# The down projection of the first feed-forward split a second time from its third block on, in a two-layer gated block on one Trainium2 core

## The chip, the cores and the metric

The kernel runs on one core of one Trainium2 chip, as one program with one launch. The metric is the device time of that core in microseconds (us). The core has a matrix engine (TensorE, PE in the profile), a vector engine (VectorE, DVE), an activation engine (ScalarE, ACT), a general one (GpSimd, POOL), and SyncE (SP), which here only issues DMA transfers. The engines run their own instruction streams, each in its order, and wait for each other through semaphores. Matrix products go into PSUM[...]; everything else lies in SBUF or, larger things, in the chip's main memory (HBM).

## The reference

The input x has 8 sequences of 512 tokens with 512 features, all in fp32. Four residual steps follow each other, each on a layer norm of x and each scaled by a learned gate:

```
x = x + tanh(g_xattn[0]) * linear_attention(layernorm(x), ctx)     # 16 heads, gated, projections 512x512
x = x + tanh(g_ffn[0])   * ffn(layernorm(x))
x = x + tanh(g_xattn[1]) * cross_attention(layernorm(x), ctx, mask)
x = x + tanh(g_ffn[1])   * experts(layernorm(x))

ffn:      h = gelu(x @ proj1.T + proj1_bias)      # 512 -> 2048
          out = h @ proj2.T + proj2_bias          # 2048 -> 512, the down projection
experts:  8 groups of a gated feed-forward, 512 -> 2 x 1536 (gate and up), silu(gate) * up,
          weighted per token by a router, then 1536 -> 512
```

All matrix products have to be as good as fp32 ones. TensorE passes each fp32 matmul twice, and the profile counts both instructions.

## The kernel before, in words

A block is one sequence of 512 tokens. The program goes through all 8 blocks of the linear attention (to about 398 us), then through the 8 blocks of the first feed-forward (`ff0`), then through the 8 blocks of cross-attention and experts (`ff1`). Between the phases each block's x goes out to HBM and comes back.

**Seven products instead of eight.** Every large matrix product is cut into 2 x 2 quarters and computed by the Strassen-Winograd scheme: seven products of sums of quarters, joined by additions. The sums on the weights' side are made once, before the phase that needs them, by a builder on POOL (`combining`, L232, four subtractions per weight tile of seven parts), and stored to HBM. The sums on the activations' side are made per block on DVE.

- An *Up unit* (`Up`, L733) takes 512 hidden features: seven products in the order 1,2,6,5,7,4,3 (`ORDER`), each 4 matmuls of 128x256 output (8 instructions, 1.73 us) with one weight tile of 256 KB. Four units make one block of `ff0`, six one of `ff1`. The matmuls are on L754.
- `Down` (L855) is the down projection of `ff0`: seven products of 16 matmuls of 128x256 (32 instructions, L870) and four weight tiles each. Its results are added onto x by DVE straight from PSUM (L886), one part of 256 tokens x 256 features at a time. `after` also makes one more sum, s2 (L889).
- `SplitDown` (L893) is the down projection of `ff1`. It cuts each of the seven products a second time into seven, so there are 49 inner products, each over three chunks of 128 rows: 21 matmuls of 128x128 output (42 instructions, L941) per outer product. `combine` (L924) makes the four inner sums of an outer operand on DVE, each of 128x384. The seven inner results of an outer product lie in two PSUM banks, four in the first and three in the second. They are first summed over the outer products (ACT copies on L957 and L958, DVE additions on L963) into `sums`, and `whole` joins the inner sums at the end of the block (three additions on L989, eight gated additions onto x on L993).

The last products of each unit (from the sixth of an Up unit and the seventh of a down projection on) are run after the first product of the next unit (`steps`, L1123), so that PE has work while other engines finish.

**Banks.** Five accumulation banks are handed out from a list, `idle_banks`; three further banks serve transposes and the like. A product's letter (x, w, z, v in the profile's names) says which accumulator it uses; products 1 and 6 of a down projection use the same one.

**Weights and queues.** All weights stream from HBM through a ring of 16 tiles of 256 KB (`load_steps`, L1284), as transfers on SP's queue; a tile is loaded again as soon as PE has read it. SP issues in program order during both feed-forwards' first part (L1343), whereas the order of the other engines' instructions is chosen by the scheduler that builds the program; from the first block of `ff1` on no engine is bound to the program's order. `load_x` brings in the x of the block after next, also on SP, at the 20th product of a block (L1405); stores of x go out on ACT's queue.

**Normalization of the next block.** Statistics on DVE (L404, L405), the reciprocal root on POOL (rstd, L411), the scaling on DVE (xn, L420), transposes on PE (L427) and copies by ACT (L430) are done piecewise during a block for the next one; then four sums S on DVE (L539 to L542). POOL adds the second bias to x (L550).

**The builder during `ff0`.** While `ff0` runs, a generator (`build_weights("ff1")`, L347, and in its wake `build_stream`, L372) makes the weights of `ff1`. One step is taken after every fourth product of a block:

```
        if k % 4 == 0:
            next(builder, None)
```

Its pool `build` has two tiles of seven parts (L1345). A step issues loads on SP, or one POOL operation, or the stores on SP. For the twice split weights each of three chunks needs a second tile, and the result goes to `stream`, in the order in which the matmuls will read it.

Of the kernel before, what the change touches and what calls it, by code (L numbers as in the profile page):

```python
# [30 lines left out]
P = 128  # L31
# [37 lines left out]
def flamingo_kernel(  # L69
# [212 lines left out]
    SPLIT_ORDER = (2, 4, 1, 6, 5, 7, 3)  # L282
    SPLIT_INNER = (1, 2, 4, 5, 6, 7, 3)
    SPLIT_CHUNKS = NJ // 4
    stream = dram.tile([P, 7, 7, SPLIT_CHUNKS, P], F32, tag="stream", name="stream")
# [61 lines left out]
    def build_weights(ph, tile7):  # L347

        todo = {
            "ff0": (("up", raw_p1, 4), ("down", raw_p2, 4)),  # L350
            "ff1": (("up", raw_gu, 6),),
        }[ph]
        todo = [(kind, raw, i) for kind, raw, n in todo for i in range(n)]

        def load(kind, raw, i):
            t = tile7(f"{ph}_{kind}{i}")
            raw(t, i)
            return t

        t = load(*todo[0])  # L360
        yield
        for n, (kind, raw, i) in enumerate(todo):
            following = load(*todo[n + 1]) if n + 1 < len(todo) else None
            yield from combining(nc.gpsimd, t)
            for q in range(7):
                nc.sync.dma_start(out=store[ph, kind, i, q], in_=t[q])
            yield
            t = following
        if ph == "ff1":
            yield from build_stream(tile7)  # L370

    def build_stream(tile7):  # L372
        place = [SPLIT_ORDER.index(m) for m in (1, 5, 2, 3, 6, 7, 4)]
        for i in range(SPLIT_CHUNKS):
            t = tile7(f"ff1_down{i}")
            w = [t[k] for k in place]
            raw_dn(w, i)
            yield
            yield from combining(nc.gpsimd, w)

            t = buildp_view(t)
            more = buildp_view(tile7(f"ff1_split{i}"))
            m = {
                1: t[:, :, 0, 0], 5: t[:, :, 0, 1], 2: t[:, :, 1, 0], 3: t[:, :, 1, 1],
                6: more[:, :, 0, 0], 7: more[:, :, 0, 1], 4: more[:, :, 1, 0],
            }
            for dst, a, b in ((7, 3, 5), (5, 5, 1), (6, 3, 5), (4, 2, 6)):
                nc.gpsimd.tensor_tensor(m[dst], m[a], m[b], ALU.subtract)
                yield
            for n, k in enumerate(SPLIT_INNER):  # L390
                nc.sync.dma_start(out=stream[:, :, n, i, :], in_=m[k])
            yield

# [499 lines left out]
    class SplitDown(Unit):  # L893
# [4 lines left out]
        kind, i = "down", 0  # L898
        order, head = SPLIT_ORDER, 6
# [4 lines left out]
        def __init__(self, ph, b, chunks):  # L904
            self.ph, self.b, self.chunks, self.tag, self.banks = ph, b, chunks, f"{ph}_{b}_down", {}
            self.combined, self.numbers = {}, {}

        def step(self, m):
            name = self.BANK[m]
            if m in self.OPENS:  # L910
                two = [acc_bank(f"{name}{k}_{self.tag}") for k in range(2)]
                self.banks[name] = [t.rearrange("p n (h q) -> p (n h) q", q=P) for t, _ in two]
                self.numbers[name] = [n for _, n in two]
            self.product(m, self.banks[name])
            self.after(m, self.banks[name])
            if m in self.CLOSES:
                idle_banks.extend(self.numbers[name])

        def quarters(self, m):

            a = inner[self.NAMES[m]].rearrange("p (k n) (t q) -> p t n k q", n=2, q=P)
            return {f"{t + 1}{n + 1}": a[:, t, n] for t in range(2) for n in range(2)}

        def combine(self, m):  # L924

            a = self.quarters(m)
            s = second.tile([P, 4, self.chunks, P], F32, tag="split", name=f"split{m}_{self.tag}", bufs=2)
            nc.vector.tensor_tensor(s[:, 0], a["21"], a["22"], ALU.add)
            nc.vector.tensor_tensor(s[:, 1], s[:, 0], a["11"], ALU.subtract)
            nc.vector.tensor_tensor(s[:, 2], a["11"], a["21"], ALU.subtract)  # L930
            nc.vector.tensor_tensor(s[:, 3], a["12"], s[:, 1], ALU.subtract)
            self.combined[m] = s

        def product(self, m, p):
            a, s = self.quarters(m), self.combined.pop(m)
            w = ring_w[self.ph, self.kind, self.b]
            operand = {1: a["11"], 2: a["12"], 4: a["22"], 5: s[:, 0], 6: s[:, 1], 7: s[:, 2], 3: s[:, 3]}
            for n, k in enumerate(SPLIT_INNER):
                for c in range(self.chunks):
                    at = (SPLIT_ORDER.index(m) * 7 + n) * self.chunks + c  # L940
                    nc.tensor.matmul(  # L941
                        p[n // 4][:, n % 4, :],
                        lhsT=operand[k][:, c, :],
                        rhs=w[at // 4][:, ts(at % 4, P)],
                        start=m in self.OPENS and n % 4 == 0 and c == 0,
                        stop=True,
                        skip_group_check=True,
                    )

        def after(self, m, p):  # L950
            if m == SPLIT_ORDER[0]:
                t = second.tile([P, 7, 4, P], F32, tag="sums", name=f"sums_{self.tag}")
                self.sums = {(r + 1, c + 1): t[:, :, 2 * r + c, :] for r in range(2) for c in range(2)}
                self.all_sums = t

            def first(part):
                nc.scalar.copy(self.sums[part][:, 0:4], p[0])  # L957
                nc.scalar.copy(self.sums[part][:, 4:7], p[1][:, 0:3])  # L958

            def more(part):  # L960
                for at, src in ((slice(0, 4), p[0]), (slice(4, 7), p[1][:, 0:3])):
                    dst = self.sums[part][:, at]
                    nc.vector.tensor_tensor(dst, src, dst, ALU.add)  # L963

            if m in (2, 4, 6, 5):
                first({2: (1, 1), 4: (2, 1), 6: (1, 2), 5: (2, 2)}[m])
            if m == 7:
                more((2, 2))
                more((2, 1))
            if m in (1, 3):  # L970
                more({1: (1, 1), 3: (1, 2)}[m])
            if m == 6:
                nc.vector.tensor_tensor(inner["s2"], inner["a12"], inner["s2"], ALU.subtract)
            last = self.b == B - 1
            if m == 3:
                pending.extend(self.whole(0, 1) if last else self.whole(None, None))
            if m == 1 and last:
                pending.extend(self.whole(0, 0))
            if m == 7 and last:
                pending.extend(self.whole(1, None))  # L980

        def whole(self, r, c):

            x5 = xs[self.ph, self.b].rearrange("p (t r) (c h q) -> p t h (r c) q", t=2, c=2, q=P)
            at = slice(0, 4) if r is None else ts(r, 2) if c is None else ds(2 * r + c, 1)
            m = {k: self.all_sums[:, n, at] for n, k in enumerate(SPLIT_INNER)}

            def onto(k, by):
                return lambda: nc.vector.tensor_tensor(m[k], m[k], m[by], ALU.add)  # L989

            def out_of(k, t, h):
                dst = x5[:, t, h, at]
                return lambda: nc.vector.scalar_tensor_tensor(dst, m[k], GATE[self.ph], dst, ALU.mult, ALU.add)  # L993

            def done():
                if (r, c) in ((None, None), (0, 1)):
                    stores.append((self.ph, self.b))

            return [
                onto(6, 1), out_of(1, 0, 0), out_of(2, 0, 0), onto(5, 6), out_of(5, 0, 1), out_of(3, 0, 1),  # L1000
                out_of(5, 1, 1), out_of(7, 1, 1), onto(7, 6), out_of(7, 1, 0), out_of(4, 1, 0), done,
            ]
# [266 lines left out]
    def units_of(ph, b):  # L1269
        if ph == "ff0":  # L1270
            return [Ff0Up(ph, b, i) for i in range(4)] + [Down(ph, b, NF // 2)]
        return [Ff1Up(ph, b, i) for i in FF1_UNITS] + [SplitDown(ph, b, NJ // 4)]
# [11 lines left out]
    def load_steps():  # L1284
        for u, m, _ in plan:
            if isinstance(u, SplitDown):
                flat = stream.rearrange("p a b c q -> p (a b c q)")
                w = ring_w.setdefault((u.ph, u.kind, u.b), [])

                while 4 * len(w) < (SPLIT_ORDER.index(m) + 1) * 7 * SPLIT_CHUNKS:  # L1290
                    at = 4 * P * len(w)
                    t = ring(f"w_{u.ph}_{u.kind}_{u.b}_{len(w)}").rearrange("p n f -> p (n f)")
                    n = min(4 * P, 49 * SPLIT_CHUNKS * P - at)
# [12 lines left out]
    down_of = {u.b: u for u, _, _ in plan if isinstance(u, SplitDown)}  # L1306

    def tiles_of(u, m):

        if isinstance(u, SplitDown):  # L1310
            n, of = SPLIT_ORDER.index(m), 7 * SPLIT_CHUNKS
# [33 lines left out]
    buildp = build.enter_context(tc.tile_pool(name="build", bufs=2, reuse_waits="tile"))  # L1345

    seven = {}

    def build_tiles(name):
        t = buildp.tile([P, 7, 2, H2], F32, tag="build", name=f"build_{name}")  # L1350
        parts = [t[:, q] for q in range(7)]
        seven[id(parts[0])] = t
        return parts

    def buildp_view(parts):
        return seven[id(parts[0])].rearrange("p k n (h q) -> p k n h q", q=P)

    pick_experts()
    builder = build_weights("ff1", build_tiles)


# [5 lines left out]
    for u, m, n in plan:  # L1367
# [7 lines left out]
        if n == 2 * B and k == 0:  # L1375
            for _ in builder:
                pass
# [8 lines left out]
        if isinstance(u, Ff1Up) and u.i == FF1_UNITS[-1]:  # L1386

            if m in (2, 7):
                down_of[u.b].combine({2: 2, 7: 4}[m])
            if m == 3:  # L1390
                down_of[u.b].combine(1)
        if isinstance(u, SplitDown) and m in (4, 1, 6, 5, 7):
            u.combine(SPLIT_ORDER[SPLIT_ORDER.index(m) + 1])
# [5 lines left out]
        if k % 4 == 0:  # L1399
# [67 lines left out]
```

## Time and profile before

| | |
|---|---|
| time, median of 3 | 2124.71 us (2124.39 to 2125.57) |
| profiled execution | 2125.65 us |
| its span, first to last instruction | 2123.8 us |
| granted TensorE clock, mean | 0.995 |
| PE busy | 2088.8 us |
| DVE busy | 1238.9 us |
| ACT busy | 555.4 us |
| POOL busy | 251.5 us |
| DMA, mean over the span | 205 GB/s |

The span is the time from the first to the last instruction on the core in one profiled execution; the time is what the device reports for a whole execution, some 2 us more. "Busy" is the time in which an engine was at work on an instruction; loading weights (PEld) overlaps with the matmuls. A group of instructions is shown by its source line, engine, operation, and output and inputs by the program's names. Lines in the profile are lines of this kernel; where a helper records an operation, its line is L60.

### The profile page before, as it was taken

What the parts mean: (1) busy time and instruction counts of PE and PEld (TensorE: products, weight loads), DVE (VectorE), ACT (ScalarE), POOL (GpSimd) and SP (SyncE); (2) the same over time, 40 slices, a digit from 0 to 9 for tenths busy, and PEclk for the clock granted to TensorE, in tenths of its full rate; (3) what the DMA queues carried; (4) which work ended last, traced back from release to release, by engine and by line L of the source; (5) the groups of instructions that cost most, each with busy time, mean ns of one, the idle gap of its engine ahead of it and who ended that gap; (6) DMA issues with size and microseconds to landing.
All of it is one profiled execution on the core that took longest, in us unless ns stands there. A gap on an engine that the chain in (4) does not pass through costs nothing.

```text
span 2123.8 us, 30856 instructions
## 1 busy us (share of the span) xinstructions
PE 2088.8 (98%) x11452; PEld 1807.3 (85%) x11452; DVE 1238.9 (58%) x2289; ACT 555.4 (26%) x1146; POOL 251.5 (12%) x228
## 2 busy tenths in 40 slices
PE   8999999999999999999999999999999999999998
PEld 4778787788888888888888889898989889898988
DVE  3687787642333323242325278777777777876857
ACT  3433333222131303031324131212222222222121
POOL 3121111330111031030301010000000010100000
PEclk9999999999999999999999999999999999999999
DMA  7345633676666665575757658677776858585865
GB/s 224 120 154 161 201 129 101 214 252 212 216 211 204 222 207 187 175 242 170 245 164 237 198 164 277 196 249 224 217 247 185 284 167 293 162 282 160 269 203 164
DMA packets 258454, 434.84 MB, mean 205 GB/s; under 512 B 34305, under 2 KB 75937, under 8 KB 254209
## 3 DMA queue, kind: packets, MB, share of 16 engines
q1 hardware_dynamic: 250864, 406.10, 61.1%
q10 hardware_dynamic: 5856, 23.20, 3.0%
q0 software_dynamic: 1584, 3.57, 0.7%
q8 instruction: 92, 1.51, 0.3%
q14 instruction: 58, 0.47, 0.1%
HBM read 369.00 MB, written 63.77 MB: 204 GB/s over the span
## 4 chain that ended last, share of the span: by engine, by line
PE 82%; issue 8%; DMA 3%; DVE 3%; POOL 2%; SPq 1%; ACT 1%; POOLq 0%; ACTq 0%; DVEq 0%
PE x_ff L754 25%; PE w_ff L754 13%; PE x_ff_down L870 10%; PE z_ff L754 6%; PE x_ff_down L941 5%; PE w_ff_down L870 5%; PE w_ff_down L941 3%; PE z_ff_down L870 3%; PE v_ff_down L941 2%; PE z_ff_down L941 2%; PE pt_ff L427 1%; SPq L60 1%; PE pt_xa L427 1%; PE pr L620 1%; PE pst L578 1%
## 5 line engine op out<-in xcount | busy, mean ns | idle before, releaser
L766 ACT COPY u_ff<-x_ff 128x512 f32<-128x512 f32 x240 | 139.6, 582 | 773.0 <-PE x_ff L754 772.9
L754 PE MATMUL x_ff<-S_ff,w_ff_up 128*128 128x256 f32 x1280 | 304.7, 381 | 1.3 <-ACT u_ff L766 1.3
L754 PE MATMUL w_ff<-S_ff,w_ff_up 128*128 128x256 f32 x1280 | 303.9, 380 | 1.0 <-DVE a_ff L809 1.0
L754 PE MATMUL x_ff<-xnT_ff,w_ff_up 128*128 128x256 f32 x1280 | 293.2, 379 | 0.0
L754 PEld LDWEIGHTS x_ff<-S_ff,w_ff_up 128*128 128x128 f32 x1280 | 239.5, 190 | 46.0 <-issue 9.9
L754 PEld LDWEIGHTS w_ff<-S_ff,w_ff_up 128*128 128x128 f32 x1280 | 239.2, 190 | 33.3 <-issue 1.4
L754 PEld LDWEIGHTS x_ff<-xnT_ff,w_ff_up 128*128 128x128 f32 x1280 | 240.0, 190 | 32.3 <-issue 0.6
L870 PE MATMUL x_ff_down<-w_ff_down,a_ff 128*128 128x256 f32 x768 | 169.7, 379 | 0.0
L870 PEld LDWEIGHTS x_ff_down<-w_ff_down,a_ff 128*128 128x128 f32 x768 | 145.9, 190 | 19.9
L886 DVE SCALAR_TENSOR_TENSOR x_ff<-x_ff_down,gates,x_ff 128x512 f32<-128x512 f32 x32 | 24.0, 750 | 221.9 <-PE x_ff_down L870 216.4
L754 PE MATMUL z_ff<-xnT_ff,w_ff_up 128*128 128x256 f32 x640 | 151.5, 379 | 0.0
L754 PEld LDWEIGHTS z_ff<-xnT_ff,w_ff_up 128*128 128x128 f32 x640 | 119.8, 190 | 15.7 <-DMA w_ff_up<-ff_up 0.4
L870 PE MATMUL w_ff_down<-w_ff_down,s_ff 128*128 128x256 f32 x512 | 113.1, 379 | 0.0
L870 PEld LDWEIGHTS w_ff_down<-w_ff_down,s_ff 128*128 128x128 f32 x512 | 97.1, 190 | 13.1
L809 DVE TENSOR_TENSOR a_ff<-w_ff,u_ff 128x512 f32<-128x512 f32 x64 | 43.8, 685 | 91.9 <-ACT u_ff L766 89.8
L814 ACT ACTIVATE a_ff<-a_ff,b_sb 128x256 f32<-128x256 f32 x128 | 58.1, 500 | 95.4 <-DVE a_ff L809 95.2
L837 DVE SCALAR_TENSOR_TENSOR g_ff<-th_ff,x_ff 128x512 f32<-128x512 f32 x48 | 32.8, 684 | 83.6 <-ACT th_ff L836 83.6
L793 DVE TENSOR_TENSOR s_ff<-a_ff,a_ff 128x512 f32<-128x512 f32 x56 | 39.9, 712 | 68.0 <-ACT a_ff L814 67.8
L550 POOL TENSOR_TENSOR x_ff<-x_ff,b_sb 128x512 f32<-128x512 f32 x28 | 36.9, 1326 | 334.7 <-DVE xn_ff L420 334.7
L847 DVE TENSOR_TENSOR up_ff<-w_ff,u_ff 128x512 f32<-128x512 f32 x96 | 65.5, 682 | 18.2 <-ACT u_ff L766 18.2
L941 PE MATMUL x_ff_down<-w_ff_down,split_ff_down 128*128 128x128 f32 x576 | 69.9, 276 | 0.0
L839 DVE TENSOR_TENSOR g_ff<-g_ff,share 128x512 f32<-128x512 f32 x96 | 67.1, 699 | 2.1
(260 smaller groups left out, 3269.2 us busy)
## 6 DMA issues: line engine op xcount, KB each, us to landing
w_ff_up<-ff_up SPq DMA_DIRECT2D x560, 256.0 KB
w_ff_down<-stream SPq DMA_DIRECT2D x288, 256.0 KB
w_ff_down<-ff_down SPq DMA_DIRECT2D x224, 256.0 KB
x_ff<-x_ff SPq DMA_DIRECT2D x16, 1024.0 KB
share<-shares SPq DMA_DIRECT2D x64, 256.0 KB
ff_up<-build_ff_up SPq DMA_DIRECT2D x42, 256.0 KB
spread<-over SPq DMA_DIRECT2D x32, 256.0 KB
x_ff<-x_xa ACTq DMA_DIRECT2D x8, 1024.0 KB
```

Of the source, the lines that this page charges most:

```text
L427: nc.tensor.transpose(pt[:, c, :], xn[t][:, ts(c, P)], ident)
L550: nc.gpsimd.tensor_tensor(xb[:, t, :], xb[:, t, :], b2_sb, ALU.add)
L754: nc.tensor.matmul(p[:, n, :], lhsT=w[:, c, ts(n, P)], rhs=moving, **self.mark(m, 2 * n + c),)
L766: nc.scalar.copy(self.s[m], p)
L793: nc.vector.tensor_tensor(s1, a21, a22, ALU.add)
L809: nc.vector.tensor_tensor(h, p, s, ALU.add)
L814: nc.scalar.activation(h[:, n, :], p[:, n, :], AF.Gelu, bias=b1_sb[:, f : f + 1])
L837: nc.vector.scalar_tensor_tensor(g, th, 1.0, p, ALU.add, ALU.mult)
L839: nc.vector.tensor_tensor(g, g, share, ALU.mult)
L847: nc.vector.tensor_tensor(u, p, s, ALU.add)
L870: nc.tensor.matmul(p[:, t, :], lhsT=a[:, k, ts(t, P)], rhs=w[k // 2][:, k % 2, :], **self.mark(m, 2 * k + t),)
L941: nc.tensor.matmul(p[n // 4][:, n % 4, :], lhsT=operand[k][:, c, :], rhs=w[at // 4][:, ts(at % 4, P)], start=m in self.OPENS and n % 4 == ...
```

## The change

From the third block on (`ONCE = 2`), `ff0` uses `SplitDown` too. The class serves both phases, with its own order of outer products and number of chunks for each (four for `ff0`, three for `ff1`). In `ff0` an outer product is 28 matmuls of 128x128 (56 instructions), its inner sums are of 128x512, and a down projection reads 49 weight tiles of 256 KB where `Down` reads 28.

In `ff0` the seven inner results of an outer product are joined by themselves (`at_once`): ACT copies the two banks to two temporary tiles, DVE makes the joins in six additions, and one or two parts of x get the results by two gated additions each.

The weights for this, `stream["ff0"]`, are made during the first two blocks of `ff0` by a builder called `again`, one step after every second product; the builder of `ff1` follows it, one step after every fourth. Both now work in place, in one tile (`bufs=1`), with two POOL operations in a step (`in_twos`). The raw load of the next tile is issued when the stores of the one before have been issued.

The inner sums of an operand come from a pool of seven single tiles (`splits`) in place of two tiles of four. In both phases they are made one outer product ahead (`step`); for `ff1` this moves the sums of the first outer operands, which were made during the last Up unit.

The seven inner results have new places (`SPLIT_SLOT`): results 1, 6, 2 and 3 lie in the first bank, 4, 5 and 7 in the second, whereas the order in which they are computed stays 1,2,4,5,6,7,3. Joining in `ff1` uses the same six additions and two gated additions (`joined`), each over the four parts of x at once, where `whole` had three and eight.

```diff
-    SPLIT_ORDER = (2, 4, 1, 6, 5, 7, 3)
+    SPLIT_ORDER = {"ff0": (1, 4, 2, 6, 5, 7, 3), "ff1": (2, 4, 1, 6, 5, 7, 3)}
+    SPLIT_CHUNKS = {"ff0": NF // 4, "ff1": NJ // 4}
     SPLIT_INNER = (1, 2, 4, 5, 6, 7, 3)
+    SPLIT_SLOT = {1: 0, 6: 1, 2: 2, 3: 3, 4: 4, 5: 5, 7: 6}
+    ONCE = 2
...
+    def build_stream(ph, raw, tile7):
+        place = [SPLIT_ORDER[ph].index(m) for m in (1, 5, 2, 3, 6, 7, 4)]
+        for i in range(SPLIT_CHUNKS[ph]):
+            t = tile7(f"{ph}_down{i}")
+            w = [t[:, k] for k in place]
+            raw(w, i)
             yield
+            yield from in_twos(combining(nc.gpsimd, w))
...
+            for m, w in ((1, b11), (2, b21), (3, b22)):
+                keep(m, w)
             yield
+            nc.gpsimd.tensor_tensor(b12, b12, b11, sub)
+            keep(5, b12)
+            yield
+            nc.gpsimd.tensor_tensor(b22, b22, b12, sub)
+            keep(6, b22)
+            yield
+            nc.gpsimd.tensor_tensor(b21, b21, b22, sub)
+            nc.gpsimd.tensor_tensor(b11, b22, b11, sub)
+            keep(4, b21)
+            keep(7, b11)
+            yield
+        streamed.add(ph)
...
+            n = self.order.index(m) + 1
+            if n < 7:
+                self.combine(self.order[n])
...
-            s = second.tile([P, 4, self.chunks, P], F32, tag="split", name=f"split{m}_{self.tag}", bufs=2)
+            s = [
+                splits.tile([P, self.chunks, P], F32, tag="split", name=f"split{m}{k}_{self.tag}", bufs=7)
+                for k in range(4)
+            ]
...
+                    bank, place = divmod(SPLIT_SLOT[k], 4)
                     nc.tensor.matmul(
-                        p[n // 4][:, n % 4, :],
+                        p[bank][:, place, :],
...
+        def joined(self, m):
+            def onto(k, by):
+                return lambda: nc.vector.tensor_tensor(m(k), m(k), m(by), ALU.add)
+            rows = slice(SPLIT_SLOT[2], SPLIT_SLOT[3] + 1), slice(SPLIT_SLOT[4], SPLIT_SLOT[5] + 1)
+            first = m(slice(SPLIT_SLOT[1], SPLIT_SLOT[6] + 1))
+            ops = [onto(6, 1), onto(7, 6), onto(6, 5)]
+            ops.append(lambda: nc.vector.tensor_tensor(m(rows[0]), m(rows[0]), first, ALU.add))
+            return [*ops, onto(4, 7), onto(5, 7)], [m(r) for r in rows]
...
+        def at_once(self, m, p, parts):
+            t = [temp(f"part{m}{k}_{self.tag}").rearrange("p (s q) -> p s q", q=P) for k in range(2)]
+            nc.scalar.copy(t[0], p[0])
+            nc.scalar.copy(t[1][:, 0:3], p[1][:, 0:3])
...
+            for op in ops:
+                op()
+            xb = xs[self.ph, self.b]
+            for r, c in parts:
+                for n in range(2):
+                    self.gated(xb[:, 2 * (r - 1) + n, ts(c - 1, H2)], rows[n])
...
+            if self.ph == "ff0":
+                parts = {1: [(1, 1)], 2: [(1, 1)], 4: [(2, 1)], 6: [(1, 2)], 3: [(1, 2)], 5: [(2, 2)]}
+                self.at_once(m, p, parts.get(m, [(2, 2), (2, 1)]))
...
-            return [Ff0Up(ph, b, i) for i in range(4)] + [Down(ph, b, NF // 2)]
+            return [Ff0Up(ph, b, i) for i in range(4)] + [Down(ph, b, NF // 2) if b < ONCE else SplitDown(ph, b)]
...
-    buildp = build.enter_context(tc.tile_pool(name="build", bufs=2, reuse_waits="tile"))
+    splits = stack(tc.tile_pool(name="splits", bufs=1, reuse_waits="tile"))
+    buildp = build.enter_context(tc.tile_pool(name="build", bufs=1, reuse_waits="tile"))
...
-        if isinstance(u, Ff1Up) and u.i == FF1_UNITS[-1]:
-            if m in (2, 7):
-                down_of[u.b].combine({2: 2, 7: 4}[m])
-            if m == 3:
-                down_of[u.b].combine(1)
-        if isinstance(u, SplitDown) and m in (4, 1, 6, 5, 7):
-            u.combine(SPLIT_ORDER[SPLIT_ORDER.index(m) + 1])
+        if isinstance(u, Ff1Up) and u.i == FF1_UNITS[-1] and m == 2:
+            down_of["ff1", u.b].combine(2)
+        if isinstance(u, Ff0Up) and u.i == 3 and m == 7 and u.b >= ONCE:
+            down_of["ff0", u.b].combine(1)
...
-        if k % 4 == 0:
+        ticks += 1
+        if ticks % 2 == 0 and "ff0" not in streamed:
+            next(again, None)
+        elif ticks % 4 == 0:
             next(builder, None)
```

## The prediction

> **What bounds the kernel now.** I read the busy totals first, then the chain that ended last, then busy time by stretch, then the pieces of that chain inside each stage. Totals and chain:
>
> ```profile
> PE 2088.8 (98%) x11452; PEld 1807.3 (85%) x11452; DVE 1238.9 (58%) x2289; ACT 555.4 (26%) x1146; POOL 251.5 (12%) x228
> PE 82%; issue 8%; DMA 3%; DVE 3%; POOL 2%; SPq 1%; ACT 1%; POOLq 0%; ACTq 0%; DVEq 0%
> ```
>
> TensorE is busy for 2088.8 of 2123.8 us, so only fewer or shorter matmuls can shorten the middle of the kernel by much. The stretches show it per block (columns: stretch, busy us and instructions of PE, weight load, DVE, ACT, POOL; granted clock; DMA share; GB/s):
>
> ```profile
> 447.73:546.18 98.45, 98.45 (x465) 86.69 (x465) 31.17 (x51) 22.73 (x48) 16.51 (x14) 1.00 0.71 226
> 841.53:941.51 99.98, 98.72 (x465) 86.60 (x465) 29.47 (x47) 22.71 (x48) 17.68 (x12) 1.00 0.68 213
> 941.51:1041.20 99.69, 99.69 (x471) 87.78 (x471) 29.28 (x43) 23.33 (x49) 14.55 (x11) 1.00 0.66 205
> 1041.20:1149.75 108.55, 106.70 (x538) 89.89 (x537) 42.54 (x95) 35.35 (x73) 12.42 (x12) 1.00 0.58 177
> ```
>
> Each of the first three is one block of the first feed-forward. The first is all PE. The second lost 1.26 us (the load of x landed late: DVE waited 6.7 us for it), the fourth, where the second feed-forward begins, 1.85 us (a rstd on POOL stood behind the builder of weights). DVE has 67 us free per block, and DMA moves 205 to 226 GB/s. Now the two kinds of down product, one line from the first feed-forward and two from the second (start, us, what):
>
> ```profile
> 654.99 6.91 PE z_ff_down L870 x32
> ...
> 1280.48 4.69 PE z_ff_down L941 x42
> 1288.74 4.69 PE v_ff_down L941 x42
> ```
>
> A 256-column matmul instruction takes 6.91/32 = 0.216 us, a 128-column one 4.69/42 = 0.1117 us: half the columns cost 52% of the time, not 50. The second form runs without a gap between pieces, and this is the form that the first feed-forward is to take over.
>
> [...]
>
> **The change, part by part.**
>
> *Matmuls.* A block's down projection was 7 products of 32 instructions: 7 x 6.907 = 48.35 us. With a second split in four chunks it is 7 x 56 instructions x 0.1117 = 43.79 us. That is 4.56 us less per block, for six of eight blocks: **-27.4 us**. Nothing else of PE's is removed.
>
> *DVE.* The rows that price what is added (by shape; busy, mean ns):
>
> ```profile
> L928 DVE TENSOR_TENSOR split_ff_down<-a_ff 128x384 f32<-128x384 f32 x40 | 22.0, 550 | 0.2
> L989 DVE TENSOR_TENSOR sums_ff_down<-sums_ff_down 128x128 f32<-128x128 f32 x6 | 1.7, 285 | 0.0
> L989 DVE TENSOR_TENSOR sums_ff_down<-sums_ff_down 128x256 f32<-128x256 f32 x3 | 1.3, 421 | 0.1
> L993 DVE SCALAR_TENSOR_TENSOR x_ff<-sums_ff_down,gates_half,x_ff 128x256 f32<-128x256 f32 x8 | 3.7, 480 | 0.1
> ```
>
> Per block: 28 operand sums of 128x512 at 0.69 us (a 128x512 tensor_tensor in other rows) are 19.3 us, or 17 if they run back to back, where they start 0.60 us apart. Joining a product at once is 5 x 0.285 + 0.421 + 2 x 0.480 = 2.81 us, and 0.96 more for product 7, which goes onto two parts: 7 x 2.81 + 0.96 = 20.6 us. The old seven additions (0.75 us each) go: -5. So 31 becomes about 65 us of a block of 93.9: no bound over the block. But nearly all of it falls into the down phase: 17 to 19 for operands, 20.6 for joins, 2.3 for s2, and some 4 to 5 for the next block's normalization and S, together 44 to 47 us in the 43.8 us of products and the first Up products beside them. Joins may lag, since TensorE waits for operands only; I walked DVE's issue order against the times at which PE needs each operand and found at least 2.4 us to spare at each product, least at the fourth operands of products 5 and 7. That walk assumes nothing upstream late. In the changed order the next block's statistics (which wait for its load of x) and xn (which waits for rstd on POOL) stand before or among the first splits. Each lateness beyond some 3 us is PE time. Bounds: 0 to 2 us a block, 12 in all; not below nothing, as nothing on PE gets shorter by it. I take **+5**.
>
> *ACT.* Two copies per product, 0.58 + 0.48 us, 7.4 us per block; ACT is busy 22.7 of 98 and its copies free the banks 1.1 us after a product. The next product starts in a free bank and comes to a reused one only two sevenths (1.8 us) later, so nothing. If that cover went, 1.1 us x 7 per block would be.
>
> *Weights and DMA.* A down phase loads 49 tiles of 256 KB, not 28. With 28 Up tiles that is 77, or 20.2 MB; x in and out is 2.1 MB, the builder about 6: 28.5 MB in 93.9 us, 304 GB/s. The first stretch shows 226 GB/s at share 0.71, so full engines give 318 of this mix; the second feed-forward reaches more:
>
> ```profile
> 1410.00:1420.00 10.00, 10.00 (x90) 9.87 (x89) 10.00 (x19) 1.06 (x2) 0.00 (x0) 1.00 1.00 322
> 1420.00:1430.00 10.00, 10.00 (x84) 9.79 (x84) 7.05 (x14) 1.38 (x3) 0.00 (x0) 1.00 1.00 362
> ```
>
> TensorE stays at 10.00 of 10 there, so full queues alone don't stop it: the ring of 16 tiles is 28 us of Up products and 14 us of split ones. I take **0**, with rival B for the rest.
>
> *Builder.* The new stream is made in blocks 0 and 1, every second tick: per chunk 1 MB read, 3.1 MB written and POOL 4 x 1.35 + 4 x 2.08 = 13.7 us, in 7 steps of 3.5 us. POOL has over 80 us free per block. One tile is in use instead of two, so each raw load waits until the stores before it have landed, on SP, ahead of the ring's loads; stores wait on POOL's last op, again on SP. Such a wait is 2 to 4 us against 28 us of ring: hidden. Afterwards the second feed-forward's builder steps every fourth tick (45 steps, 180 ticks, done by block 7).
>
> *Moved slots.* In the second feed-forward products 1 and 6 share the x banks. The first bank now holds inner sums that are written until product 1 ends (inner order 1,2,4,5,6,7,3 writes banks 0,0,1,1,0,1,0), where before it was complete after four sevenths. So 6 must wait for DVE to read that bank (0.69 us), which was hidden by the last three sevenths. In the changed order PE has five short matmul groups between them, about 1.1 us: 0 to 0.85 us per block, more if DVE is late. **+1.5** over eight.
>
> *Joins of the second feed-forward.* Six sums and two gated steps instead of three and eight: 8.0 becomes 7.3 us per block, under a PE that never stops, so 0. At the end of the kernel it does count. The chain's last pieces before:
>
> ```profile
> 2118.28 1.15 DVE x_ff L993 x4
> ...
> 2119.78 0.36 DVE x_ff L993
> ...
> 2120.17 0.35 DVE x_ff L993
> ```
>
> The last part took 3 x 0.285 + 8 x 0.346 = 3.6 us and will take 2.8: **-1**, with the copies' order. It can't lose more than the half microsecond by which a 128x256 step is longer.
>
> *Old losses.* The 1.26 and 1.85 us are ties of queues, redrawn by the change: between both kept and both gone (0 to -3.1). I take **-1.6**.
>
> Sum: -27.4 + 5 + 1.5 - 1 - 1.6 = -23.5. The profiled execution took 2125.65 us for its span of 2123.8, 0.9 us over the median of 2124.71; less 23.5 it gives 2102.1 profiled, and **2101** from the median, which I predict.
>
> **Rivals.**
>
> A: DVE sets the pace of ff0's down phases. For: 44 to 47 us of work in 44 us, and an x load that already came 2 to 7 us late for DVE in blocks before. Against: 2.4 us to spare, joins can lag into 48 us of Up products with little DVE work. At 2 to 4 us per block: 12 to 24 us, so 2108 to 2120.
>
> B, the other side: DMA cannot bring 304 GB/s. A block no faster than 98.45 us means 28.5 MB/98.45 = 290 GB/s; below that rate the change loses. At 270 a block takes 105.6 us, and the five blocks with a builder give 36 us more than before, less 4.6 for the last: about 2156. At 285, 100.0 us: 5 x 1.55 - 4.6 = 3, about 2128. For: [...]one queue in program order, and SP waits on POOL in front of ring loads. Against: 322 and 362 above, and a 318 scaled from this very stage.
>
> C: bank waits between products 1 and 6 in full, 8 x 0.85 = 7 us, instead of 1.5: 2107.
>
> D: the pace isn't kept, so the change doesn't do what it says: with weight loads of 0.19 us beside 128-column matmuls, any slip shows at once. If an instruction takes 0.117 us, a block gains 2.5 us: 15 in all, 2113. Against: 0.1117 is measured on the same form, over 2352 instructions, with operands from the same kinds of buffers.
>
> **How the numbers follow.** My case (2095 to 2109) 0.60, A 0.16, B 0.11, C 0.07, D 0.06. Up to 2120 all but B and an exceptional A are in; the low end is no stall, both old losses gone: 2124.7 - 27.4 - 1 - 3.1 = 2093. Range 2093 to 2120. About 0.2% (4.2 us) is what a measurement tells from no change: faster 0.87 (all but B and the worst of A), same 0.03, slower 0.10.
>
> **What would show it.** Right: down products of 6.25 us x56 in six blocks; PE busy in them equal to the stretch within 1 us; block pitch 93.9 instead of 98.5; PE's instructions up by 6 x 7 x 24 = 1008; last DVE pieces of 0.48 us. Wrong: PE waiting for DVE's split sums in the down phase (A); PE waiting for DMA of w_ff_down with DMA share near 1.00 (B); PE waiting for DVE's sums before product 6 in the second feed-forward (C); pieces of x56 longer than 6.3 us with no wait named (D). A stall in blocks 0 or 1, where only the builder is new, would upset the step on the builder.

## The result and the profile after

The changed kernel takes 2112.51 us (median of 5 runs, 2107.20 to 2114.74) against 2124.44 us before. The ratio is 0.9939, with a 95% interval of 0.9924 to 0.9953, so it is faster by 11.9 us. The forecast was 2101, with a range of 2093 to 2120: the sign and the range hold, but the gain is half of the 23.5 us that the sum gave.

The profiled execution is the fastest of the five runs: 2107.20 us, span 2105.4, mean granted clock 0.997. The other four have a clock of 0.993 to 0.995. That difference returns below.

The page of the changed kernel, busy time by engine and the chain that ended last:

```profile
PE 2064.2 (98%) x12460; PEld 1813.6 (86%) x12460; DVE 1435.2 (68%) x2701; ACT 594.3 (28%) x1230; POOL 319.5 (15%) x260
...
PE 73%; issue 9%; DVE 6%; DMA 5%; POOL 4%; SPq 1%; ACT 1%; POOLq 0%; DVEq 0%; ACTq 0%
```

PE has exactly 1008 instructions more, as worked out, and 24.6 us less to do. But its share of the chain fell from 82 to 73%, and DVE's and POOL's shares rose from 3 and 2 to 6 and 4%. So something now stands in PE's way that did not before. Pieces of the chain in the second twice split block (start, us, what):

```profile
765.18 6.25 PE x_ff_down L979 x56
771.44 6.25 PE w_ff_down L979 x56
```

A product takes 6.25 us where it took 6.91, which is the 56 x 0.1117 us of the forecast. The matmuls' gain is there. The time that is missing shows in the stretches of the first feed-forward (columns as before: stretch, busy us and instructions of PE, weight load, DVE, ACT, POOL; clock; DMA share; GB/s):

```profile
600.00:700.00 100.00, 98.34 (x653) 91.66 (x653) 67.17 (x130) 29.26 (x62) 18.12 (x13) 1.00 0.89 295
700.00:800.00 100.00, 98.80 (x657) 91.87 (x656) 67.53 (x130) 31.27 (x66) 23.06 (x18) 1.00 0.92 310
800.00:900.00 100.00, 97.05 (x643) 89.83 (x642) 68.90 (x129) 30.71 (x65) 27.00 (x14) 1.00 0.87 288
900.00:1000.00 100.00, 98.68 (x653) 91.77 (x652) 69.57 (x130) 30.90 (x66) 24.94 (x15) 1.00 0.88 291
```

PE idles for 7.1 us in these 400, in which the second feed-forward's weights are made beside the split down projections. From 1000 to 1100 us, where the builder comes to its end, it loses nothing. What PE waited for from 600 to 1100 us (us in total, times, longest):

```profile
PE z_ff_down L979 <- DVE a_ff L839: 2.9, 2, 1.7
PE x_ff_down L979 <- DVE split_ff_down L967: 2.5, 2, 1.3
PE x_ff_down L979 <- DVE split_ff_down L966: 1.0, 1, 1.0
PE w_ff_down L979 <- DVE split_ff_down L967: 0.7, 1, 0.7
```

Each wait is for DVE, inside a down projection, 7 to 38 us after it began: once for an operand of its first product, twice for one of the third, three times for those of the fourth and fifth. Whether DVE is late for its own work, for a late x, for slow tiles, or for something that holds it, these lines don't say. The next view does: DVE's and POOL's instructions at 853 to 865 us (start, us, engine, line, what):

```profile
853.17 6.35 POOL L414 TENSOR_TENSOR build_ff_down<-build_ff_down 128x896 f32<-128x896 f32 x1 [5.63 <-DMA stream_ff<-build_ff_down]
...
859.59 2.41 POOL L417 TENSOR_TENSOR build_ff_down<-build_ff_down 128x896 f32<-128x896 f32 x1
...
859.99 2.17 DVE L993 TENSOR_TENSOR part_ff_down<-part_ff_down 128x128 f32<-128x128 f32 x1
861.97 2.12 POOL L418 TENSOR_TENSOR build_ff_down<-build_ff_down 128x896 f32<-128x896 f32 x1
862.08 2.56 DVE L966 TENSOR_TENSOR split_ff_down<-s_ff 128x512 f32<-128x512 f32 x1
```

A DVE addition of 128x128 takes 2.17 us, where 0.28 is the median of its row. It began while a subtraction of the builder ran on POOL, and ended within 0.2 us of it. The 128x512 sum behind it takes 2.56 us in place of 0.68, beside the next subtraction. And POOL's own 128x896 subtraction took 6.35 us, where 2.08 is usual, while DVE had a row of additions to do.

These are not single cases. From 600 to 1100 us the trace has 503 additions and subtractions on DVE (TENSOR_TENSOR). 442 of them had no instruction of POOL beside them, and none of these took over 1.3 times the median of its kind. 26 of the others did, and each of the 26 had a subtraction of the builder or an addition of the second bias beside it on POOL.

Which part of the chip the two engines contend for no trace here shows. What the trace shows is the durations and the count above, and the prediction had not reckoned with them.

### The profile page after: what moved, and what is told of

It reads as the page before. It is cut to its first block, busy times and chain, and to the rows that moved or that the text cites. A ratio compares the mean times of both kernels' runs of the same rounds, so it can differ in the third digit from the quotient of the medians.

```text
span 2105.4 us, 34132 instructions
## 1 busy us (share of the span) xinstructions
PE 2064.2 (98%) x12460; PEld 1813.6 (86%) x12460; DVE 1435.2 (68%) x2701; ACT 594.3 (28%) x1230; POOL 319.5 (15%) x260
## 4 chain that ended last, share of the span: by engine, by line
PE 73%; issue 9%; DVE 6%; DMA 5%; POOL 4%; SPq 1%; ACT 1%; POOLq 0%; DVEq 0%; ACTq 0%
PE x_ff L784 23%; PE w_ff L784 11%; PE x_ff_down L979 9%; PE w_ff_down L979 7%; PE z_ff L784 6%; PE z_ff_down L979 3%; PE v_ff_down L979 3%; PE x_ff_down L900 2%; PE w_ff_down L900 1%; SPq L60 1%; PE pt_ff L457 1%; PE pt_xa L457 1%; PE pr L650 1%; DMA stream_ff<-build_ff_down 1%; PE pst L608 1%
## 5 line engine op out<-in xcount | busy, mean ns | idle before, releaser
L784 PEld LDWEIGHTS x_ff<-S_ff,w_ff_up 128*128 128x128 f32 x1280 | 239.4, 190 | 44.8 <-issue 10.3
L979 PE MATMUL x_ff_down<-w_ff_down,split_ff_down 128*128 128x128 f32 x1152 | 136.6, 275 | 4.1 <-DVE split_ff_down L967 2.5
L979 PEld LDWEIGHTS x_ff_down<-w_ff_down,split_ff_down 128*128 128x128 f32 x1152 | 132.4, 192 | 4.8 <-DVE split_ff_down L967 2.9
L839 DVE TENSOR_TENSOR a_ff<-w_ff,u_ff 128x512 f32<-128x512 f32 x64 | 43.8, 684 | 74.1 <-ACT u_ff L796 74.1
L979 PE MATMUL w_ff_down<-w_ff_down,split_ff_down 128*128 128x128 f32 x768 | 90.6, 275 | 0.7 <-DVE split_ff_down L967 0.7
L979 PEld LDWEIGHTS w_ff_down<-w_ff_down,split_ff_down 128*128 128x128 f32 x768 | 88.1, 192 | 0.9 <-DVE split_ff_down L967 0.9
L993 DVE TENSOR_TENSOR part_ff_down<-part_ff_down 128x128 f32<-128x128 f32 x210 | 64.3, 322 | 21.0 <-ACT part_ff_down L1006 16.7
L450 DVE TENSOR_SCALAR xn_ff<-x_ff,mv_ff,rstd_ff 128x512 f32<-128x512 f32 x64 | 41.6, 666 | 42.0 <-PE pt_ff L457 30.1
L979 PE MATMUL w_ff_down<-w_ff_down,s_ff 128*128 128x128 f32 x576 | 70.2, 275 | 0.0
```

What stands on the lines that cost most here:

```text
L450: nc.vector.tensor_scalar(xn[t], xb[:, t, :], mv[:, t, 0:1], rstd[:, t : t + 1], ALU.subtract, ALU.mult)
L784: nc.tensor.matmul(p[:, n, :], lhsT=w[:, c, ts(n, P)], rhs=moving, **self.mark(m, 2 * n + c),)
L839: nc.vector.tensor_tensor(h, p, s, ALU.add)
L979: nc.tensor.matmul(p[bank][:, place, :], lhsT=operand[k][:, c, :], rhs=w[at // 4][:, ts(at % 4, P)], start=bank not in opened, stop=True, ...
L993: return lambda: nc.vector.tensor_tensor(m(k), m(k), m(by), ALU.add)
```

## The experiments

Four theories were set against each other. **Port**: the builder's subtractions on POOL hold DVE (the word is a name for this theory; no run shows at what they hold it). **Queue**: POOL is busy with the builder, and rstd comes late behind it. **Load**: DVE's own 45 us in a down phase are too much (the first rival of the prediction). **DMA**: tiles or x come late.

**Fills in place of POOL's subtractions.**

```diff
-            yield from in_twos(combining(nc.gpsimd, t))
+            yield from in_twos(filling(t))
...
+    def filling(w):
+        for k in (5, 1, 4, 6):
+            nc.gpsimd.memset(w[k], 0.01)
+            yield
```

The four subtractions of the second split are replaced in the same way.

> The changed kernel with the arithmetic of the second feed-forward's builder replaced: in place of each subtraction, POOL fills the same tile with a constant, which reads nothing from SBUF; loads, stores and their order stay. Left out: the Winograd sums of the second feed-forward's weights, so its outputs are of other weights. Theory port[...]: DVE's long instances (128x128 additions of up to 2.2 us, 128x512 ones of 1.7 to 2.6) go from blocks 4 to 6, and of the 7.3 us that PE lost more in the first feed-forward than before, 4 to 7 come back: about 2106 against 2112.5. Theory load (DVE's own 45 us in a down phase are the bound) and theory DMA (tiles or x late): unchanged within 2 us, about 2112.

Measured: 2100.29 us (2098.51 to 2101.62), ratio to before 0.9885 (0.9868 to 0.9901). That is 12.2 us below the changed kernel, more than the theory had asked for. The two profiled executions lie only 6.9 us apart (2100.31 and 2107.20), close to the 7.1 us that PE idles in these stretches of the changed kernel; the rest of the 12.2 lies in executions of the changed kernel that no trace shows. The same stretches:

```profile
600.00:700.00 100.00, 100.00 (x664) 93.30 (x663) 62.72 (x130) 30.90 (x65) 12.16 (x16) 1.00 0.91 302
700.00:800.00 100.00, 100.00 (x661) 92.89 (x660) 62.16 (x130) 32.25 (x68) 12.28 (x15) 1.00 0.93 313
800.00:900.00 100.00, 100.00 (x662) 93.08 (x661) 64.23 (x133) 32.44 (x69) 13.84 (x16) 1.00 0.90 300
900.00:1000.00 100.00, 100.00 (x664) 93.08 (x663) 62.68 (x130) 32.16 (x69) 14.66 (x16) 1.00 0.85 286
```

PE is full in all four, with about the same number of DVE instructions and GB/s. DVE is busy for 251.8 us here and for 273.2 in the changed kernel: the 21 us between them were not work, but time in which it was held. That rules out the theory of DVE's own load. The other weights that this kernel computes with don't explain it either: in both kernels a block of the second feed-forward, which uses them, takes 115.62 us from the second block to the seventh. A fill is also shorter than a subtraction, 0.52 against 1.35 us, so queue was still open.

**As busy, with fills.** The same kernel with each fill done three times.

```diff
-            nc.gpsimd.memset(w[k], 0.01)
+            for _ in range(3):
+                nc.gpsimd.memset(w[k], 0.01)
```

> As the first experiment (fills in place of the builder's subtractions in the second feed-forward's weights, its outputs are of other weights), but each fill is done three times, so that POOL is about as long busy with the builder as in the changed kernel (3 x 0.52 us for 1.35, 3 x 0.84 for 2.1), and rstd stands as long behind it. Theory port: the fills read nothing, so DVE isn't held, and it stays near 2100 (2098 to 2104). Rival theory queue (POOL busy, rstd late behind the builder): back to 2110 to 2114.

Measured: 2101.64 us (2100.81 to 2108.59), ratio 0.9899 (0.9880 to 0.9919). Its page:

```profile
PE 2064.7 (98%) x12460; PEld 1814.4 (86%) x12460; DVE 1409.8 (67%) x2701; ACT 595.7 (28%) x1230; POOL 319.5 (15%) x356
```

POOL is busy for 319.5 us, as in the changed kernel, and the gain stays. PE waits for nothing between 600 and 1100 us. So it isn't that POOL is busy, nor that rstd stands behind its work. 71 additions of DVE ran beside a fill alone in this stretch, and the longest took 1.03 times the median of its kind: what held DVE's additions in the changed kernel comes with the subtractions, which have two inputs in SBUF, and not with the fills, which have none. The bias additions, which stayed, still held 8 additions of DVE, and PE had time for that.

**Half of the stream.** Every second tile of the first feed-forward's split weights isn't loaded.

```diff
+                    if u.ph == "ff0" and len(w) % 2:
+                        w.append(w[-1])
+                        yield
+                        continue
```

> The changed kernel, but of the first feed-forward's twice split weights only every second tile is loaded and used twice: 25 tiles a block in place of 49, so 6.3 MB less in each of six blocks, about 237 GB/s in place of 304. Left out: half of the weights, so the values are others; all matmuls and all DVE work stay. Theory DMA: PE's waits in the first feed-forward go and the time falls by 6 us or more, to 2106 or below. Theories port and load: unchanged within 3 us, 2110 to 2114, since neither POOL nor DVE has less to do.

Measured: 2111.37 us (2110.07 to 2117.05), ratio 0.9936 (0.9919 to 0.9952), the ratio of the changed kernel. DMA moves 210 to 238 GB/s in the four stretches in place of 288 to 310, and PE still waits for DVE's sums (10.1 us from 600 to 1100 in the profiled execution, the slowest of the four). The theory of DMA falls for these stalls.

**Never split.**

```diff
-    ONCE = 2
+    ONCE = B
...
-    streamed = set()
+    streamed = {"ff0"}
```

> The changed kernel without its main part: the first feed-forward's down projection stays split once in all blocks and its twice split stream is not made (the constant for the first block is 8); slots, joins and the builder in place stay. If the rest is worth what the prediction said (joins -1, wait between products 1 and 6 +1.5, old losses between 0 and -3), 2122 to 2126; the split itself is then the difference to 2112.5, about 10 to 13 net of its stalls. If the bank wait in the second feed-forward costs its full 7 us, about 2131.

Measured: 2121.80 us, ratio 0.9986 (0.9979 to 0.9993), so all that is not the split is worth -3.0 us. Its stretches between 400 and 1100 us have PE at 100.00 of 100, where the kernel before lost 1.26 to a late x. The split itself is then worth about 2112.5 - 2121.8 = -9.3 us net, where its matmuls alone were to give -27.4.

**The builder elsewhere.** Two ways of moving its steps were to keep POOL's subtractions away from the down phases. First, steps in Up units alone:

```diff
-        elif ticks % 4 == 0:
-            next(builder, None)
+        elif u.kind == "up":
+            ups += 1
+            if ups % 3 == 0:
+                next(builder, None)
```

> The changed kernel with the second feed-forward's builder stepped only in Up units (every third product of them) and never during a down projection; same work in the same order, values unchanged. Theory port: [...]3 to 6 us come back, about 2107 to 2109. Theory load: no change, 2112. Theory DMA: the builder's 6 MB per block move out of the down phase, where the stream needs 292 GB/s, so 2 to 6 us come back as well.

Measured: 2115.35 us, ratio 0.9956 (0.9942 to 0.9970): no better than the changed kernel, with 9.1 us of waits from 600 to 1100 us for the last Up unit's `a_ff` and for split sums. The edit did not do what it was meant to. A step that is taken in an Up unit only puts its work in POOL's order. POOL does it when what stands before it is done and its transfers have landed, here after the down projection had begun at 836.7 us:

```profile
846.43 2.41 POOL L417 TENSOR_TENSOR build_ff_down<-build_ff_down 128x896 f32<-128x896 f32 x1
846.82 2.56 DVE L966 TENSOR_TENSOR split_ff_down<-a_ff 128x512 f32<-128x512 f32 x1
848.80 2.53 POOL L418 TENSOR_TENSOR build_ff_down<-build_ff_down 128x896 f32<-128x896 f32 x1
849.31 2.56 DVE L967 TENSOR_TENSOR split_ff_down<-a_ff,split_ff_down 128x512 f32<-128x512 f32 x1
```

Again each subtraction stretches a sum of 0.68 us, and in the next block a second group of them ran 20 to 30 us into the down projection. So this run says nothing against the theory of the port. The stall that followed shows a second cost. The chain of this kernel:

```profile
854.93 0.61 DVE a_ff L839
...
855.58 9.46 PE z_ff_down L979 x56
```

and its stretches around it:

```profile
852.00:856.00 4.00, 1.50 (x10) 1.31 (x11) 3.86 (x11) 0.44 (x2) 0.00 (x0) 0.87 0.73 248
856.00:860.00 4.00, 4.00 (x20) 4.00 (x20) 4.00 (x8) 1.32 (x4) 0.00 (x0) 0.50 0.24 66
860.00:864.00 4.00, 4.00 (x31) 4.00 (x30) 4.00 (x10) 0.00 (x0) 0.00 (x0) 0.78 0.58 156
```

PE stood still for 2.5 us, the granted clock was half from 855.0 to 861.8 us, and the product took 9.46 us in place of 6.25. A wait of 2.5 us cost 5.7.

Second, steps in the first two of four Up units alone, four per seven products.

```diff
-        elif ticks % 4 == 0:
-            next(builder, None)
+        elif u.kind == "up" and u.i < 2:
+            ups += 1
+            if ups % 7 in (0, 2, 4, 6):
+                next(builder, None)
```

> The changed kernel with the second feed-forward's builder stepped only in the first two of a block's four Up units (4 steps per 7 products there), so that neither the last Up units, in which DVE makes the statistics, xn and the first split sums, nor the down projection meet its subtractions; values unchanged. Theory port, with the place of the conflict at the turn from Up to down: 2101 to 2106. If any concentration of the builder hurts as in the run with Up units alone (2115), 2112 to 2117.

Measured: 2116.41 us, ratio 0.9958 (0.9941 to 0.9975). In the first two twice split blocks PE now loses nothing: from 600 to 800 us it is at 99.95 and 100.00. But once it waits for 7.7 us. The chain at that place:

```profile
935.08 7.24 DMA x_ff<-x_ff
...
942.34 0.03 DVE st_ff L434
...
942.95 0.69 DVE split_ff_down L964
...
943.68 1.43 PE x_ff_down L979 x5
```

The next block's x was issued at 935.08 us, about 2 us after the down projection had begun, behind twelve raw loads of the builder. Its statistics stand in front of the first split sum in DVE's order, so PE waited for an x that the next block needs. Here too the clock was halved: its mean is 0.50 from 940 to 945 us.

POOL's other additions during a down projection are the four of the second bias (1.36 us each). They were moved into the second Up unit, alone and together with the early builder.

```diff
+        if isinstance(u, Ff0Up) and u.i == 1 and m in (1, 6, 7, 3) and u.b >= ONCE:
+            t = (1, 6, 7, 3).index(m)
+            xb = xs["ff0", u.b]
+            nc.gpsimd.tensor_tensor(xb[:, t, :], xb[:, t, :], b2_sb, ALU.add)
```

> The changed kernel with POOL's four additions of the second bias onto x (1.36 us each, two SBUF inputs) moved for blocks from the third on from the turn between two blocks into the second Up unit of their own block; values unchanged. Theory port: these hold DVE as well, but are 5.4 us per block against 15 of the builder, so 1 to 3 us come back: 2109 to 2112. Theory queue: rstd has its place before them, so nothing, 2112.

> Both of the last two together: the builder in the first two Up units only, and the bias additions in the second. Theory port: no POOL work that reads SBUF stands at the turn from Up to down except rstd; PE waits of the first feed-forward from block 2 on below 1 us in all, 2099 to 2104. If the time is that of the early builder alone, the bias additions do not matter.

Measured: 2113.10 us (ratio 0.9938, 0.9921 to 0.9955) and 2115.92 us (0.9962, 0.9949 to 0.9974). Neither differs from the kernel that it was made from. The 1 to 3 us that had been expected of the bias are not there, as the kernel with fills suggests, and the early builder's late x remains (8.1 us in one wait).

**The load of x elsewhere.** The late x looked easy to mend. On ACT's queue:

```diff
-        queue = nc.scalar if ph == "xa0" and b > 1 else nc.sync
+        queue = nc.scalar if ph == "xa0" and b > 1 or ph == "ff0" and b > 2 else nc.sync
```

This edit stands on the early builder, then together with an early pace of the new stream's own builder, and then alone on the changed kernel:

> The early builder again (second feed-forward's builder in the first two Up units only), with one more edit: in the first feed-forward x is loaded on ACT's queue, so that it no longer stands on SP behind the builder's raw loads. In the early builder alone PE waited 7.7 us once, in the fourth twice split block, for a load of x issued at 935 us behind twelve raw loads, and the clock was halved after it. If that stall was the only thing that took back the gain: PE waits from 600 to 1100 us fall below 2 us and the time to 2102 to 2106. If the early builder has another cost (more POOL work per Up unit), it stays above 2110.

> As the one before, and the builder of the first feed-forward's stream in its blocks 0 and 1 skips the last Up unit of a block (every second product of the others). Port theory: the 1 to 3 us that PE lost between 400 and 600 us at the turn from Up to down go too: 1 to 2 us below the one before.

> The changed kernel with only the load of x moved to ACT's queue in the first feed-forward, the builder as it was. Port theory: the stalls at the turn come from POOL's reads, not from a late x, so 0 to 2 us better than 2112.5, 2110 to 2113. If x was what came late, 2105 or below.

Measured: 2124.67, 2125.34 and 2120.05 us (ratios 0.9993, 0.9994 and 0.9979; the last from 0.9967 to 0.9991). The load on ACT made both kernels slower, the early builder by 8.3 us and the changed kernel by 7.5; the pace of the new stream's builder made no difference. The trace of the last of the three, ACT's issues and its next copy:

```profile
701.59 0.33 ACTq L170 DMA_DIRECT2D x_ff<-x_ff  x1
709.22 0.33 ACTq L153 DMA_DIRECT2D x_ff<-x_ff  x1
709.64 1.07 ACT L796 COPY u_ff<-x_ff 128x512 f32<-128x512 f32 x2 [5.13 <-DMA x_ff<-x_ff]
```

The load takes the buffer of an x that had just been stored, and was issued only 7.6 us after the store. It waited on ACT, in front of a copy that frees a bank: ACT sat idle for 5.13 us, and PE waited 10.6 us for such copies from 600 to 1100. The wait had only changed its queue.

Last, the early builder with the load of x on SP as before, eight products earlier.

```diff
-        if k == 20 and n + 2 < 3 * B:
+        if k == (12 if n < 2 * B else 20) and n + 2 < 3 * B:
```

> The early builder (second feed-forward's builder in the first two Up units only), with the load of x on SP as before, but issued after the 12th product of a block of the first feed-forward in place of the 20th, so that it stands in front of most of the builder's transfers; values unchanged. If the one late x (7.7 us, and the halved clock after it) was what took back the early builder's gain, PE waits from 600 to 1100 us fall below 2 us and the time to 2102 to 2107, below both kernels. If moving the load makes SP wait for the store of the x before it (as ACT did when the load stood there), 2112 or above.

Measured: 2135.15 us, ratio 1.0048 (1.0036 to 1.0060), slower than the kernel before. The load was issued 20 to 25 us ahead of the down phase, as meant, where the changed kernel has 6 to 12. But the scheduler moved the statistics forward in DVE's order by about as much (they stand 15 to 17 us ahead of the down phase, where the changed kernel has 1 to 6), so that they waited for x all the same. What DVE waited for between 600 and 1000 us in this kernel:

```profile
DVE st_ff L434 <- DMA x_ff<-x_ff: 26.1, 4, 7.4
```

Now additions of an Up unit stand behind that wait, and PE waited for them (11.3 us from 600 to 1100, `a_ff` L839), and 4.7 us for ACT's copies. No version that keeps the values beat the changed kernel, so the 12.2 us are shown by kernels that compute with other weights, and not yet by one that could be used.

## Why the prediction was half right

- *Matmuls, -27.4.* Right: 6.25 us for a product, 1008 instructions more. Where nothing holds PE a block takes 94.0 us from its first Up product to that of the next, against 93.9 in the forecast and 98.5 before: four blocks in a row in the kernel with fills, the last of the four in the changed kernel. The three before it took 95.5 to 97.8.
- *Everything beside the split.* The sum had -1 for the joins at the end, +1.5 for products 1 and 6, and -1.6 for old losses: -1.1. The kernel that never splits gives -3.0. The old losses in the first feed-forward went entirely there, and the bank wait is smaller than the 1.5 us: a block of the second feed-forward takes 115.62 us where it took 115.53, and in the changed kernel's block at 1275 us PE goes from product 1 to 6 with four instructions and 0.03 us between. The gain at the end hardly came. From the start of the last matmul to the end of the span it is 8.3 us before and 8.2 after; DVE ends 0.2 us earlier after it.
- *DVE, +5 (0 to 12).* This step failed. 12.2 us came back when the second feed-forward's builder filled in place of subtracting, as much as the whole term was to cost at most, and in all the split fell short by 27.4 - 9.3 = 18 us in the typical run. The amount of work was right: the forecast had 65 us of 93.9 per block, and the kernel with fills shows 62 to 64 per 100. The walk through DVE's order, with 2.4 us to spare at each product, used durations that a free DVE has and asked what could make its inputs late. It did not ask what could make its own instructions longer, and the profile before shows that something does. In its third block, where `s_ff` sums have a median of 0.69 us:

```profile
612.65 1.60 POOL L237 TENSOR_TENSOR build_ff_up<-build_ff_up 128x512 f32<-128x512 f32 x1
613.16 1.64 DVE L794 TENSOR_TENSOR s_ff<-s_ff,a_ff 128x512 f32<-128x512 f32 x1
```

It cost nothing then, since DVE had 67 us free per block and PE hardly ever waited for it.

- *The builder, "hidden".* The same miss from the other side. I priced POOL's time and SP's waits, and found cover for both. The cover for this conflict was DVE's free time, 67 us of a block; the change leaves 30 to 33 of 100.
- *How the 18 us are made up.* 12.2 are the builder's subtractions. For the other 6 there is only the profile of the kernel with fills, and no experiment. It shows 2.3 us lost between 400 and 600, where the new stream's subtractions still run on POOL, and 2.0 us more than the never-split kernel between 1100 and 1160, most of it one wait of 2.0 us for xn that the changed kernel has there too. After that wait the clock was half for 3.4 us, an estimated 1.7 us; in the changed kernel's profile the wait was not followed by it.
- *The rivals.* The time lies where the first rival put it (2108 to 2120), and the sign named for it came, PE waiting for DVE's split sums. But its mechanism, DVE's own work as the pace, is excluded: with the same work and fills in place of the builder's subtractions, PE loses nothing (400.00 of 400 us). That the stated range held is in part luck: it reached so far up for this rival, while the cost came from something that no rival names. DMA (the second) is excluded for these stalls by the halved stream, the full bank wait (the third) and a slower pace (the fourth) by the trace.
- *The spread.* The runs before lie within 1.2 us, those after within 7.5. The cause is open, since only the fastest was profiled, and with it 5.3 of the 12.2 us. That standstills of 2 to 2.5 us are sometimes followed by a halved clock in other traces, and that the slower runs have the lower mean clock, points to it. But the mean also counts the start of the program: the kernel with fills had 0.995 at 2100.3 us.

## What to carry to other kernels

An engine with much of its time free, as DVE had with 67 of 98 us here, covers not only its own delays but also conflicts that nobody sees. Before filling that time, look at how long its instructions become at their longest, and what runs on the other engines at that moment. A median or a mean over a group hides it: 0.284 us is the median of a row whose longest was 2.17. A step that is moved in the program has not moved in time until the trace shows it. And a wait moved to another queue is gone only if nothing urgent stands behind it there.

## What the runs showed of the hardware

- A builder's subtraction on POOL held a two-input addition on DVE for up to 1.9 us (2.17 for 0.28, 2.56 for 0.68), and DVE's additions held POOL (6.35 for 2.08). Beside fills on POOL, as busy for as long, no addition took over 1.03 times its median, and the whole took 2101.6 in place of 2112.5 us.
- The scaling xn, with one tensor and two columns as inputs, was held as well, by a subtraction (2.30 us for 0.55, at 934.4 us of the changed kernel) and even by a fill (1.04 us, at 927.1 us of the kernel with single fills).
- PE's granted clock can halve after a standstill of only 2.0 us. In the kernel with single fills PE stood still from 1101.9 to 1103.8 us, and the clock was half from 1104.6 to 1108.0; in the changed kernel the same standstill, from 1110.8 to 1112.7, was followed by a full clock. After 2.5 us in the kernel with steps in Up units, a product of 6.25 us took 9.46. The halved stretches after these standstills lasted 3.4 and 6.8 us. In the run with half of the stream, where PE was busy for 1.16 of the 4 us from 650 on, it was 3.4 us (a mean clock of 0.57 from 654 to 658), and in the early builder, where PE waited for 7.7 us, 10.3 (0.92, 0.50 and 0.55 in the three stretches of 5 us from 935 to 950). What decides whether a standstill is followed by a halved clock these runs don't show.
